# One-hots placed later on VectorE, more gathered rows issued by SyncE, and a joined end in a graph layer

## The chip, the cores and the metric

The kernel runs on one core of one Trainium2 chip. The engines of the core are TensorE (PE in the profile; PEld is its weight load), VectorE (DVE), ScalarE (ACT), GpSimd (POOL) and SyncE (SP), which only issues DMAs and waits. The metric is the device time of one launch in microseconds. Before the change it is 1567.36 us, the median of 3 runs (1563.31 to 1572.13).

## The reference

A graph layer with a residual and a layer norm. There are 6250 nodes with 64 features and 200000 edges, sorted by destination:

```python
w   = silu(edge_attr_32 @ W1 + b1) @ W2 + b2              # per edge, 9 weights
msg = einsum('ef,em,fmg->eg', x[src], edge_attr_9 * w, W_tp)
agg = segment_sum(msg, dst, 6250) / sqrt(16)
emb = silu(node_vec[:, None] @ Wn1 + bn1) @ Wn2 + bn2
gamma, beta = split(emb, 2, axis=-1)
y   = x + agg * (1 + gamma) + beta
out = (y - mean(y)) / sqrt(var(y) + 1e-5)                 # over the 64 features
```

## The kernel before

**Tiles and groups.** Edges come in tiles of 128 (one edge per partition), 1563 of them, and 16 tiles make a group (the last, group 97, has 11). There are 98 groups. Nodes come in 49 blocks of 128.

**The source rows.** For each tile the 128 rows `x[src]` have to lie in the tile `hs` of the group. There are three ways to get them. Most tiles are gathered by POOL with one indirect DMA each (`gather`, L91). Three or four tiles of each group are picked on PE (`pick`, L475): one-hot matrices `hot_k`, made on DVE from the keys (`hots`, L460), multiply a copy of `x` that stays in SBUF, in 14 matmuls per tile, and two DVE instructions (L484, L486) select the row out of the result. And the first tile of every sixth group from 7 on (`SPG`, 16 groups) is fetched row by row by SyncE: `load_rows` reads the source numbers from the SBUF tile `src_r` into registers, up to eight words with one register load (L101), and then issues one DMA of 256 bytes per row (L106). It does 22 rows (`SPR`) in each of the six steps before the group is used.

**A step.** The loop `for i in range(NBLK)` writes out the order by hand for all engines, and each engine takes its own instructions in that order. Step i starts the gathers of group i+6, loads edge data `ea` and `sh` for groups i+2 and i+3 (even i; L371, L373), keys (odd i; L391), and SyncE's rows, all in SyncE's one queue apart from the gathers. DVE makes the one-hots of group i+2 (two of them first, then the rest after the first pick). PE picks the tiles of group i+1; between the matmuls of the first pick it runs `nodes(i)`: the gate of a node block (L589, read by DVE in L355 and L356, until step 50), the placing of the sums of two groups on their nodes (`place`, L559, read by DVE in L565 and ACT in L568) in even steps, and the transposing back and the finish of two node blocks (`bring`, L576, and `finish_nodes`, L669 to L683) in every fourth step. Then come the hidden layer of group i+2 (`hidden`, L403, with the SiLU L411 on ACT), the second layer of group i+1 (`second`, L420), the edge sums of group i (`windows`, L504, copied out of PSUM by ACT in L514), in odd steps the product with `W_tp` for two groups (`project`, L543 or, for a single group, L538), and the remaining picks.

**Buffers that tie the engines.** PSUM tile `s` holds the results of `nodes` and then those of `second`, one after the other, so `second` waits until DVE and ACT have read what `nodes` left. PSUM tile `p1` holds the hidden layer and then the result of `project`, so `project` waits until ACT has applied the SiLU. `hs` has 7 buffers, `ea` and `sh` 3, `hot_k` 7.

**The end.** The last groups are 96 and 97. Groups 95 and 96 make a pair; group 97 stands alone. In the last step the pair is projected, placed, brought back and finished; then `windows(97)` and a second, shorter chain for group 97 follow.

Of the kernel before, what the change touches and what calls it, by code (L numbers as in the profile page):

```python
# [7 lines left out]
F32 = mybir.dt.float32  # L8
# [19 lines left out]
LB = 2  # L28
Q = 4
J = 7  # L30
SPG = range(7, NBLK, 6)
SPR = 22
EPS = 1e-5

KH = 8
# [9 lines left out]
def pair(q):  # L45

    return [g for g in (2 * q - 1, 2 * q) if 0 <= g < NBLK]
# [12 lines left out]
def gnn_resnorm_kernel(ctx: ExitStack, tc: tile.TileContext, x, src, dst, dst_row, ea, sh, cn,  # L60
# [18 lines left out]
    with ExitStack() as fast:  # L79
# [16 lines left out]
        src_r = keep.tile([len(SPG), P], I32)  # L96

        def load_rows(g, e0):
            for e in range(e0, min(e0 + SPR, P), 8):
                n = min(8, min(e0 + SPR, P) - e)  # L100
                _, vs = nc.values_load_multi_w_load_instructions(  # L101
                    src_r[SPG.index(g):SPG.index(g) + 1, e:e + n], engines=[mybir.EngineType.SP],
                    min_val=0, max_val=NPAD - 1,
                    skip_runtime_bounds_check_because="src is below N, as for the gathers")
                for k in range(n):
                    nc.sync.dma_start(hs[g][e + k:e + k + 1, 0, :], x[bass.ds(vs[k], 1), :])  # L106
# [27 lines left out]
        def setup(temp):  # L134
# [126 lines left out]
            def between(h):  # L261

                if h == 0:
                    p_f = psum.tile([KB, NBLK], F32, tag="s", name="p_f")
                    nc.tensor.matmul(p_f, first_t, ident[0:NBLK, 0:NBLK], start=True, stop=True)
                    nc.scalar.copy(first_f, p_f)
                elif h == 1:
                    keys(0)
                    hots(0, 0, Q)
                elif h == 3:  # L270
                    p_cn = psum.tile([P, NJ], F32, tag="s", name="p_cn")
                    nc.tensor.matmul(p_cn, cn_j, ident[0:NJ, 0:NJ], start=True, stop=True)
                    cn_s = temp.tile([P, NJ], F32)
                    nc.scalar.copy(cn_s, p_cn)
                    nc.sync.dma_start(cn_d, cn_s)
                    nc.sync.dma_start(wn1c, wn1.rearrange("o h -> h o"))
                    nc.sync.dma_start(bn1c, bn1.unsqueeze(1))
                    gate_load(0)
                    nc.sync.dma_start(wn2a[0:H, :], wn2)
                    nc.sync.dma_start(wn2a[H:H + 1, :], bn2.unsqueeze(0))  # L280
                    for q in range(2):
                        n = (M + 1 - q) // 2
                        nc.sync.dma_start(wtc2[q * F:(q + 1) * F, 0:n, :], wtp[:, q:M:2, :])
                    load(LB)
                    with nc.allow_non_contiguous_dma(reason="2048 words, once"):
                        nc.sync.dma_start(src_r, src[:, SPG[0] * KB:NBLK * KB:6 * KB].rearrange("p g -> g p"))


            for h in range(J):
# [67 lines left out]

        out_v = out.rearrange("(j p) f -> p j f", p=P)

        def finish(j0, j1, sums):  # L360
            y = late.tile([P, j1 - j0, F], F32, tag="y", name=f"y{j0}")
            finish_nodes(nc, late, eps, sums, y, gam[:, j0:j1, :], xb[:, j0:j1, :], out_v[:, j0:j1, :], j0)


        ea_t, sh_t, oh_t, kr_t, st, a, zs = {}, {}, {}, {}, {}, {}, {}
# [128 lines left out]
        def windows(g):  # L494

            nk = tiles(g)
            hsg, ag = hs.pop(g), a.pop(g)
            z = zs[g] if g in zs else sums(g)
            for k0 in range(0, nk, ZT):
                n = min(ZT, nk - k0)  # L500
                pz = psum.tile([P, ZT // 2, M, W], F32, tag="pz", name=f"pz{g}_{k0}", bufs=2)
                for k in range(n):
                    v = k % 2
                    mm = nc.tensor.matmul(pz[v * F:(v + 1) * F, k // 2].rearrange("p m w -> p (m w)"),  # L504
                                          hsg[:, k0 + k, :], ag[:, k0 + k].rearrange("p m w -> p (m w)"),
                                          start=True, stop=True)
                    if k0 + k == 0:

                        for d in hs_dma.pop(g)[(g not in SPG):]:
                            tc.add_manual_dep(mm.ins, d.ins.name, mybir.DependencyInfo(  # L510
                                mybir.DependencyClass.Sync, mybir.DependencyReason.DATA), reason="rows of the group")
                for v in range(2):
                    for h in range(2):
                        nc.scalar.copy(  # L514
                            z[h * F:(h + 1) * F, 0:5 - h, k0 + v:k0 + n:2, :].rearrange("p m k w -> p k m w"),
                            pz[v * F:(v + 1) * F, 0:(n + 1 - v) // 2, h:M:2, :])

# [12 lines left out]
        def project(q):  # L530


            gs = pair(q)
            pt = psum.tile([P, 2, 4 * P], F32, tag="p1", name=f"pt{q}")
            z = [zs.pop(g).rearrange("p c k w -> p c (k w)") for g in gs]
            if len(gs) == 1:
                for c in range(5):
                    nc.tensor.matmul(pt[:, 0, 0:F], z[0][:, c], wtc2[:, c, :], start=(c == 0), stop=(c == 4))  # L538
                halves(q, pt[:, 0, 0:F].unsqueeze(1))
                return []  # L540
            for c in range(5):
                for h in range(2):
                    nc.tensor.matmul(pt[h * F:(h + 1) * F, 0, 0:P], wtc2[:, c, :], z[h][:, c],  # L543
                                     start=(c == 0), stop=(c == 4))
# [6 lines left out]

            return [lambda: None, lambda: None, turn]

        def place(q, pd):

            gs = pair(q)

            def part(k):
                nc.tensor.matmul(pd, r[q][:, k].rearrange("p s f -> p (s f)"), hot.pop(gs[k]),  # L559
                                 start=(k == 0), stop=(k == len(gs) - 1))  # L560
                if k == len(gs) - 1:
                    r.pop(q)
                    if q > 0:
                        yt[q - 1] = work.tile([P, P], F32, tag="yt", name=f"yt{q}", bufs=3)
                        nc.vector.tensor_add(yt[q - 1], pd[:, 0:P], carry.pop(q - 1))  # L565
                    if q < NJ:
                        carry[q] = work.tile([P, P], F32, tag="carry", name=f"carry{q}")
                        nc.scalar.copy(carry[q], pd[:, P:2 * P])  # L568

            return [lambda k=k: part(k) for k in range(len(gs))]  # L570

# [28 lines left out]
        with tc.manual_schedule(), tc.tile_pool(name="temp", bufs=1) as temp:  # L600
            setup(temp)

            for i in range(NBLK):
                if i + AHEAD < NBLK:
                    gather(i + AHEAD)
                if i % LB == 0 and i + LB < NBLK:
                    if i > 0:
                        load(i + LB)
                    near(i + LB)
# [2 lines left out]
                if i % 4 == 3 and i + 1 < NJ:  # L612
                    gate_load(i + 1)
                for g in SPG:
                    if 0 < g - i <= AHEAD:
                        load_rows(g, (AHEAD - g + i) * SPR)
                if i + 2 < NBLK:
                    keys(i + 2)
                    hots(i + 2, 0, 2)
                pick(i + 1, 0, [nodes(i)])  # L620
                if i + 2 < NBLK:
                    hots(i + 2, 2, Q)
                if 3 <= i <= 5:
# [4 lines left out]
                    second(i + 1)  # L628
                if i < NBLK - 2:
                    windows(i)  # L630
                turn = project(i // 2) if i % 2 == 1 else []
                if i % 4 == 1 and i - 1 < NJ:
                    gate_hidden(i - 1)
                if i + 1 < NBLK:
                    pick(i + 1, 1, [weights(i + 1), turn])
                for t in range(2, Q):
                    pick(i + 1, t)
                if i == NBLK - 1:
                    for f in turn:
                        f()  # L640
                    ps = psum.tile([P, 4, P], F32, tag="s", name="ps_l")
                    for f in place(i // 2, ps[:, 0:2].rearrange("p a n -> p (a n)")):
                        f()
                    py = psum.tile([P, FB, F], F32, tag="r", name="py_l")
                    for f in bring(NJ - 3, NJ - 1, py):
                        f()
                if i >= NBLK - 2:
                    windows(i)
                if i == NBLK - 2:
                    sums(i + 1)  # L650
            project(NBLK // 2)
            ps = psum.tile([P, 4, P], F32, tag="s", name="ps_n")
            for f in place(NBLK // 2, ps[:, 0:2].rearrange("p a n -> p (a n)")):
                f()
            for f in bring(NJ - 1, NJ, psum.tile([P, 1, F], F32, tag="r", name="py_n")):
                f()


    bad_n = nc.values_load(flag_i[0:1, 0:1], min_val=0, max_val=4 * P,
# [3 lines left out]
                     gam, xb, eps, out)  # L663


def finish_nodes(nc, work, eps, sums, y, gam, xb, out, tag):

    n = y.shape[1]
    nc.vector.tensor_mul(y, sums, gam)  # L669
# [10 lines left out]
    nc.vector.reciprocal(var, var)  # L680
    o = work.tile([P, n, F], F32, tag="o", name=f"o{tag}")
    nc.vector.tensor_mul(o, y, var.unsqueeze(2).to_broadcast([P, n, F]))
    nc.sync.dma_start(out, o)  # L683


def general_path(tc, dram, x, dst_row, ea, sh, src_i, dst_i, w1bd, b1c, w2bd, b2r, wtc,
# [3 lines left out]
    with ExitStack() as ctx:  # L690
# [109 lines left out]
        for j0 in range(0, NJ, JC):  # L800
# [4 lines left out]
            nc.vector.tensor_add(a[0], a[0], a[1])  # L805
            nc.vector.tensor_add(a[2], a[2], a[3])
            nc.vector.tensor_add(a[0], a[0], a[2])
            finish_nodes(nc, work, eps, a[0], a[0], gam[:, js, :], xb[:, js, :], out_v[:, js, :], f"g{j0}")


# [47 lines left out]
```

## Time and profile before

| | us |
|---|---|
| median of 3 runs | 1567.36 |
| the profiled execution | 1570.09 |
| its span, first to last instruction | 1568.3 |
| PE busy in it | 1460.5 |
| POOL busy | 1129.5 |
| DVE busy | 1139.5 |
| ACT busy | 528.6 |

The profile is of one execution. Its page gives busy times by engine, the groups of instructions by line with their mean duration, and the idle time before them with what ended it. A row of the waits reads: who waited, for whom, microseconds in total, times, longest. A row of the timeline reads: start, duration, engine, line, operation, output and input, number of merged instructions, and in brackets the idle time of the engine before it and what ended it. `SPq` is SyncE's queue; its instructions are not counted as busy, so its load has to be worked out from its waits and from the spacing of its instructions. The mean granted clock of PE was 0.972 of full speed.

### The profile page before, as it was taken

How to read it: one execution, taken by the hardware profiler on the slowest of the kernel's cores; microseconds unless marked ns; L12 is line 12 of the kernel's file. 1: busy time of each engine (PE TensorE's matmuls, PEld its weight loads, DVE VectorE, ACT ScalarE, POOL GpSimd, SP SyncE). 2: the span in 40 equal slices, each digit the busy share in tenths (PEclk: the TensorE clock that was granted, in tenths of full speed). 3: DMA queues.
4: the chain of work that ended last, by engine and by line, in shares of the span. 5: the costliest groups of instructions: out<-in, count | busy, mean ns of one | idle time of the engine just before them, and what ended most of it. 6: DMA issues, size and time to landing. Idle time of an engine off the chain costs nothing.

```text
span 1568.3 us, 34363 instructions
## 1 busy us (share of the span) xinstructions
PE 1460.5 (93%) x10810; PEld 1208.6 (77%) x10810; DVE 1139.5 (73%) x1987; ACT 528.6 (34%) x1335; POOL 1129.5 (72%) x1201
## 2 busy tenths in 40 slices
PE   4998999999999999999999999999999999999995
PEld 2787778778787788787877877877877878778774
DVE  5686777777777777777777777777777677777773
ACT  4232242433332423332333323323233332333331
POOL 7777777777777777777777777777777777777700
PEclk9999999999999999999999999999999999999997
DMA  5321222222222222222222222222222222222200
GB/s 166 93 62 55 53 75 51 63 56 71 57 62 65 63 54 61 56 71 59 58 71 53 59 53 71 59 53 70 53 60 55 68 54 58 71 53 59 71 7 5
DMA packets 90939, 96.16 MB, mean 61 GB/s; under 512 B 37161, under 2 KB 51451, under 8 KB 90748
## 3 DMA queue, kind: packets, MB, share of 16 engines
q1 hardware_dynamic: 51842, 53.09, 11.5%
q0 software_dynamic: 38144, 39.14, 11.4%
q8 instruction: 88, 1.44, 0.4%
q10 hardware_dynamic: 762, 1.64, 0.3%
q14 instruction: 103, 0.84, 0.2%
HBM read 92.04 MB, written 1.73 MB: 60 GB/s over the span
## 4 chain that ended last, share of the span: by engine, by line
PE 51%; POOL 20%; DVE 13%; issue 8%; DMA 4%; ACT 3%; SPq 0%; DVEq 0%; POOLq 0%; ACTq 0%
PE px L475 37%; POOL hs L91 20%; DVE hot_k L460 5%; PE pz L504 5%; DMA hs<-in_x_dram,src_i 4%; PE pt L543 3%; PE p L420 2%; DVE xm L484 2%; DVE hs L486 2%; PE p L403 1%; PE p L430 1%; ACT L411 1%; ACT st L411 1%; DVE oh L382 1%; ACT carry L568 1%
## 5 line engine op out<-in xcount | busy, mean ns | idle before, releaser
L91 POOL DMA_INDIRECT hs<-in_x_dram,src_i x1192 | 1128.2, 946 | 364.0 <-issue 335.0
L475 PE MATMUL px<-xs,hot_k 128*128 128x448 f32 x4970 | 1100.8, 375 | 8.4 <-DVE xs L294 7.8
L475 PEld LDWEIGHTS px<-xs,hot_k 128*128 128x128 f32 x4970 | 903.3, 190 | 96.7 <-issue 12.2
L484 DVE SCALAR_TENSOR_TENSOR xm<-li,jl,px 128x448 f32<-128x448 f32 x355 | 240.4, 677 | 220.2 <-PE px L475 217.9
L460 DVE TENSOR_TENSOR hot_k<-pk,nk 128x896 fp32r<-128x896 f32 x355 | 370.5, 1081 | 2.3 <-ACT pk L454 2.3
L486 DVE TENSOR_REDUCE hs<-xm 128x64 f32<-128x448 f32 x355 | 220.1, 620 | 12.5 <-DVE xm L484 0.2
L514 ACT COPY zt<-pz 64x160 f32<-64x160 f32 (+2 forms) x784 | 213.3, 272 | 23.0 <-PE pz L504 13.9
L411 ACT ACTIVATE st<-p,b1c 128x1024 f32<-128x1024 f32 x98 | 109.2, 1114 | 296.1 <-PE p L403 295.8
L568 ACT COPY carry<-ps 128x128 f32<-128x128 f32 x48 | 12.7, 265 | 390.2 <-DVE yt L565 382.4
L436 DVE TENSOR_TENSOR p<-p,sh 128x72 f32<-128x72 f32 x196 | 47.3, 241 | 132.7 <-ACT rt L546 47.7
L504 PEld LDWEIGHTS pz<-a,hs 128*64 128x64 f32 x3126 | 110.6, 142 | 41.9 <-issue 38.4
L442 DVE TENSOR_TENSOR a<-oh,p 128x1152 f32<-128x1152 f32 x98 | 132.6, 1353 | 3.3
L504 PE MATMUL pz<-a,hs 128*64 128x72 f32 x3126 | 125.5, 236 | 1.1 <-DMA hs<-in_x_dram,src_i 0.6
L403 PE MATMUL p<-ea,w1bd 64*128 64x512 f32 x392 | 113.5, 656 | 0.0
L420 PEld LDWEIGHTS p<-st,w2p 128*32 128x32 f32 x784 | 16.6, 108 | 113.3 <-issue 52.7
L543 PE MATMUL pt<-zt,wtc 128*64 128x128 f32 x960 | 72.8, 305 | 27.7 <-ACT st L411 26.0
L420 PE MATMUL p<-st,w2p 128*32 128x256 f32 x784 | 63.7, 395 | 35.7 <-DVE xb L356 32.0
L543 PEld LDWEIGHTS pt<-zt,wtc 128*64 128x64 f32 x960 | 62.2, 157 | 29.7 <-ACT st L411 27.8
L679 ACT ACTIVATE var<-var,eps 128x2 f32<-128x2 f32 (+1 forms) x25 | 7.4, 296 | 220.5 <-DVE var L678 220.5
L430 PE MATMUL p<-ident,p2s 128*128 128x128 f32 x196 | 54.4, 278 | 0.0
L454 ACT CAST pk<-kr 128x384 f32<-128x384 f16 (+1 forms) x98 | 53.9, 550 | 1.5 <-DMA kr<-kd 1.4
L403 PEld LDWEIGHTS p<-ea,w1bd 64*128 64x128 f32 x392 | 30.2, 188 | 28.8 <-issue 27.9
(122 smaller groups left out, 530.0 us busy)
## 6 DMA issues: line engine op xcount, KB each, us to landing
hs<-in_x_dram SPq DMA_DIRECT2D x2048, 0.2 KB
ea<-in_ea_dram SPq DMA_DIRECT2D x49, 512.0 KB
hs<-in_x_dram,src_i POOLq DMA_INDIRECT x1192
kr<-kd SPq DMA_DIRECT2D x49, 256.0 KB
sh<-in_sh_dram SPq DMA_DIRECT2D x49, 144.0 KB
cb<-cn_d SPq DMA_DIRECT2D x12, 128.0 KB
out_dram<-o SPq DMA_DIRECT2D x24, 64.0 KB
gam<-in_x_dram ACTq DMA_DIRECT2D x2, 448.0 KB
```

The costliest lines, as they stand in the source:

```text
L91: hs_dma[g] = [nc.gpsimd.indirect_dma_start(out=hs[g][:, t - g * KB, :], out_offset=None, in_=x, in_offset=bass.IndirectOffsetOnAxis(ap=sr ...
L403: nc.tensor.matmul(p1[:, i, :], w1bd[i * 64:(i + 1) * 64, :], e[i * 64:(i + 1) * 64, :], start=True, stop=True)
L411: nc.scalar.activation(st[g], p1_t.pop(g), AF.Silu, bias=b1c)
L420: nc.tensor.matmul(p2[g][c * D:(c + 1) * D, 0, :].rearrange("p (i e) -> p i e", i=2), w2p, s[:, :, c * P:(c + 1) * P], start=True, stop=True)
L442: nc.vector.tensor_mul(a[g], oh_t.pop(g)[:, :, None, :].to_broadcast([P, KB, M, W]), sw.unsqueeze(3).to_broadcast([P, KB, M, W]))
L460: nc.vector.tensor_tensor(hot_k[g, t], pk_t[g][:, t, None, :].to_broadcast([P, J, P]), nk.unsqueeze(2).to_broadcast([P, J, P]), op=ALU.is_ ...
L475: nc.tensor.matmul(px.rearrange("p f l -> p (f l)"), hot_k[g, t][:, h, :], xs[i][:, h].rearrange("p f l -> p (f l)"), start=(h == 0 and i ...
L484: nc.vector.scalar_tensor_tensor(xm, li[:, None, :].to_broadcast([P, F, J]), jl[:, c:c + 1], px, op0=ALU.is_equal, op1=ALU.mult)
L486: nc.vector.tensor_reduce(hs[g][:, tiles(g) - q + t, :], xm, AX.X, ALU.add)
L504: mm = nc.tensor.matmul(pz[v * F:(v + 1) * F, k // 2].rearrange("p m w -> p (m w)"), hsg[:, k0 + k, :], ag[:, k0 + k].rearrange("p m w -> ...
L514: nc.scalar.copy(z[h * F:(h + 1) * F, 0:5 - h, k0 + v:k0 + n:2, :].rearrange("p m k w -> p k m w"), pz[v * F:(v + 1) * F, 0:(n + 1 - v) // ...
L543: nc.tensor.matmul(pt[h * F:(h + 1) * F, 0, 0:P], wtc2[:, c, :], z[h][:, c], start=(c == 0), stop=(c == 4))
```

## The change

Five things are changed, and nothing else in the computation. First, the first two one-hots of a step are issued on DVE behind the work of `nodes`: the list `more` is run within `pick` after the parts of `nodes(i)`. Second, SyncE fetches the first tile of every fifth group (19 groups), 26 rows a step in five steps, with up to 13 words per register load (two loads a step); POOL gathers three tiles fewer. Third, the stores of finished blocks are put on a list and issued at the head of the next step. Fourth, `place` reads the carry with ACT ahead of DVE's addition, and the single-group `project` uses the PSUM tile `r`. Fifth, at the end the edge sums of groups 96 and 97 are made one behind the other, with half of their PSUM copies on DVE, the three remaining tiles of group 97 ahead of its first eight; then both are projected, placed into one PSUM tile, and the last three node blocks are brought back, finished and stored at once.

```diff
-SPG = range(7, NBLK, 6)
-SPR = 22
+SPG = range(7, NBLK, 5)
+SPR = 26
...
         def load_rows(g, e0):
-            for e in range(e0, min(e0 + SPR, P), 8):
-                n = min(8, min(e0 + SPR, P) - e)
+            for e in range(e0, min(e0 + SPR, P), SPR // 2):
+                n = min(SPR // 2, min(e0 + SPR, P) - e)
...
+            o = finish_nodes(nc, late, eps, sums, y, gam[:, j0:j1, :], xb[:, j0:j1, :], j0)
+            stores.append(lambda: nc.sync.dma_start(out_v[:, j0:j1, :], o))
...
-            for k0 in range(0, nk, ZT):
+            for k0 in reversed(range(0, nk, ZT)) if nk < KB else range(0, nk, ZT):
...
-                        nc.scalar.copy(
+                        (nc.vector.tensor_copy if v and g >= NBLK - 2 else nc.scalar.copy)(
...
             if len(gs) == 1:
+                pr = psum.tile([P, 1, F], F32, tag="r", name=f"pr{q}")
...
-        def place(q, pd):
+        def place(q, pd, last=None):
...
+                if last:
+                    nc.tensor.matmul(pd[:, P:2 * P], r.pop(last)[:, 0].rearrange("p s f -> p (s f)"),
+                                     hot.pop(pair(last)[0])[:, 0:P], start=False, stop=True)
+                    yt[q] = work.tile([P, P], F32, tag="yt", name=f"yt{last}", bufs=3)
+                    nc.scalar.copy(yt[q], pd[:, P:2 * P])
+                else:
+                    carry[q] = work.tile([P, P], F32, tag="carry", name=f"carry{q}")
+                    nc.scalar.copy(carry[q], pd[:, P:2 * P])
+                if q > 0:
+                    yt[q - 1] = work.tile([P, P], F32, tag="yt", name=f"yt{q}", bufs=3)
+                    nc.vector.tensor_add(yt[q - 1], pd[:, 0:P], carry.pop(q - 1))
...
                 if i + AHEAD < NBLK:
                     gather(i + AHEAD)
+                while stores:
+                    stores.pop(0)()
...
                 for g in SPG:
-                    if 0 < g - i <= AHEAD:
+                    if 0 < g - i <= AHEAD and (AHEAD - g + i) * SPR < P:
                         load_rows(g, (AHEAD - g + i) * SPR)
+                more = []
                 if i + 2 < NBLK:
                     keys(i + 2)
-                    hots(i + 2, 0, 2)
-                pick(i + 1, 0, [nodes(i)])
+                    more = [lambda: hots(i + 2, 0, 2)]
+                pick(i + 1, 0, [nodes(i), more])
...
-                if i == NBLK - 2:
-                    sums(i + 1)
+
+            turn = project(NBLK // 2 - 1)
             project(NBLK // 2)
-            ps = psum.tile([P, 4, P], F32, tag="s", name="ps_n")
-            for f in place(NBLK // 2, ps[:, 0:2].rearrange("p a n -> p (a n)")):
+            for f in turn:
                 f()
-            for f in bring(NJ - 1, NJ, psum.tile([P, 1, F], F32, tag="r", name="py_n")):
+            ps = psum.tile([P, 2 * P], F32, tag="s", name="ps_n")
+            py = psum.tile([P, 3, F], F32, tag="r", name="py_n")
+            for f in place(NBLK // 2 - 1, ps, NBLK // 2) + bring(NJ - 3, NJ, py):
                 f()
```

## The prediction

> **What bounds the kernel now.** I read the page first (busy times), then the waits of PE, then the timeline of one second-half block, then, because the change gives it work, the waits of SyncE's queue and its register loads one by one.
>
> ```profile
> PE 1460.5 (93%) x10810; PEld 1208.6 (77%) x10810; DVE 1139.5 (73%) x1987; ACT 528.6 (34%) x1335; POOL 1129.5 (72%) x1201
> ```
> ```profile
> PE p L420 <- DVE xb L356: 32.0, 34, 2.2
> PE pt L543 <- ACT st L411: 26.0, 12, 2.2
> ```
> PE has the work: 1460.5 of 1568.3 us. Its idle time inside the run comes in two repeated gaps. Until block 50, `second` (L420) waits for DVE to finish reading the PSUM tile that it wants (xb L356): some 24 times 0.38 us and 11 times 2.1 us. After that, `project` (L543) waits 12 times 2.16 us for the SiLU L411, which frees its PSUM tile. The timeline shows why:
>
> ```profile
> 1450.76 2.08 DVE L460 TENSOR_TENSOR hot_k<-pk,nk 128x896 fp32r<-128x896 f32 x2
> 1452.75 0.28 DVE L669 TENSOR_TENSOR y<-ps,gam 128x128 f32<-128x128 f32 x1
> ...
> 1454.89 0.30 ACT L679 ACTIVATE var<-var,eps 128x2 f32<-128x2 f32 x1 [7.85 <-DVE var L678]
> 1455.21 1.28 ACT L411 ACT_TABLE_LOAD   x1
> 1456.50 1.11 ACT L411 ACTIVATE st<-p,b1c 128x1024 f32<-128x1024 f32 x1
> 1457.67 1.31 PE L543 MATMUL pt<-zt,wtc 128*64 128x128 f32 x20 [2.16 <-ACT st L411]
> ```
> Two one-hots (2.08 us) stand on DVE ahead of the finish chain, so ACT's root, the table load, the SiLU and PE are all late. The windows of the profile put the clock at 0.78 in 1457:1461 and 1.00 just before: a 2 us gap is often followed by some 3.4 us at half clock.
>
> POOL issues gathers without a pause (1192 of 0.95 us with 0.30 us between), but is off the path: its last gather (block 97) starts at 1493, and PE takes block 97 at 1550.5.
>
> SyncE is not on the page as an engine. Between its first row (57.1) and its last (1531.2):
>
> ```profile
> SPq L106 <- PE pz L504: 47.3, 15, 5.1
> SPq L683 <- DVE xb L356: 41.1, 11, 6.6
> SPq L683 <- DVE o L682: 38.6, 12, 5.8
> SPq L106 <- DVE hs L486: 4.5, 1, 4.5
> ```
> With three microseconds of small waits that is 134 us. So SyncE is occupied for 1474 - 134 = 1340 us: it has 9% of slack, and every `ea` load stands in the same queue behind the rows.
>
> **What SyncE's work costs.** Eight rows in a run, then single register loads (min/median/max ns; one instruction each):
>
> ```profile
> 1447.66 3.15 SPq L106 DMA_DIRECT2D hs<-in_x_dram  x8
> ```
> ```profile
> L101 SPq TENSOR_LOAD <-src_r x1: 732/732/732, 1440.3 to 1440.3; - x1
> L101 SPq TENSOR_LOAD <-src_r x1: 799/799/799, 1446.7 to 1446.7; - x1
> L101 SPq TENSOR_LOAD <-src_r x1: 997/997/997, 1450.8 to 1450.8; - x1
> L101 SPq TENSOR_LOAD <-src_r x1: 1932/1932/1932, 1457.2 to 1457.2; - x1
> L101 SPq TENSOR_LOAD <-src_r x1: 1987/1987/1987, 1462.6 to 1462.6; - x1
> L101 SPq TENSOR_LOAD <-src_r x1: 1567/1567/1567, 1468.0 to 1468.0; - x1
> L101 SPq TENSOR_LOAD <-src_r x1: 735/735/735, 1529.9 to 1529.9; - x1
> ```
> A row costs (3.15 - 0.23)/7 = 0.42 us. The loads are, in order, of words 0-7, 8-15, 16-21, 22-29, 30-37, 38-43, and (last line) 126-127. Eight words cost 0.73 or 1.93 us, by where they begin: words 0 and 8 lie on 16-byte bounds, words 22 and 30 do not. The slow ones fit 0.33 + 0.20 per word (2: 0.73, 6: 1.53, 8: 1.93); the quick ones fit the same with four words at the price of one (8: 0.73; 6 as 4+1+1: 0.93, measured 1.00). Traffic of the `ea` load just before does not explain it: the two-word load stands in the same kind of step and is cheap, and six quick words cost more than eight. I read it as: a start off a 16-byte bound is read word by word.
>
> **The change, part by part.**
>
> *One-hots behind the reads.* No instruction is added. In the 11 finish steps of the first half the chain starts 1.4 us earlier (it still waits for `bring`), so a gap of 2.1 leaves 0.7: 15 us. The 24 gaps of 0.38 go: 9 us. In the second half 1.87 of 2.16 goes, 12 times: 22 us. Fourteen half-clock stretches of 3.4 us cost about 1.6 each (estimate, half of 3.4): 22 us. Together up to 68 us of PE time, if nothing else is late. The one-hots are later by the 3 to 4 us of the chain, covered: they serve the next block's picks. What is late next, were PE free, is POOL.
>
> *Rows by SyncE.* POOL loses 3 gathers x 1.25 = 3.7 us. SyncE gains 3 groups x 128 = 384 rows x 0.42 = +161 us.
> Register loads: before, a group has 3 x (0.73 + 0.80 + 1.00) + 2 x (1.93 + 1.99 + 1.57) + (2.03 + 1.98 + 0.74) = 23.3 us, x16 = 373. After, a group has ten loads beginning at words 0, 13, 26, 39, 52, 65, 78, 91, 104, 117. Only 0, 52 and 104 are on a 16-byte bound. No row shows a 13-word load. Its bounds: below, three quick fours and a single, 0.33 + 4 x 0.20 = 1.1; above, 0.33 + 13 x 0.20 = 2.93 word by word. I take the upper end for the seven unaligned ones, since all four unaligned rows lie on that line, and 1.17 for the three others: 3 x 1.17 + 6 x 2.93 + 2.53 (11 words) = 23.6, x19 = 449. That is +76 for 98 loads fewer; each load less saves 0.1 of gaps, -10. At the lower end it would be about -150.
> The later issue of the stores leaves SyncE's queue as it was: a store stands ahead of the next block's loads in both. That ACT's carry now goes ahead of DVE's yt, and that the one-group project of block 1 writes another PSUM tile, I cost at nothing: the first swaps two reads of 0.27 and 0.28 us of one tile, the second happens once; without cover it is under 1 us.
> Sum on SyncE: 1340 + 161 + 76 - 10 = 1567 us, 16.5 us a step over 95 steps. PE needs 15.6 before and 14.9 with the gain. So SyncE becomes the bound, its waits vanish, and PE waits at `hidden` (L403) for `ea` every second step; the 68 us on PE are swallowed by that wait.
>
> *The Trainium skill, Runtime: NRT & Kernel Launch, section Instruction fetch mechanics, says that a register load costs about 200 ns a register even in bulk. The slope of the unaligned rows agrees (1.93 - 0.73 over six words); the aligned eight words at 0.73 do not. By that rule for all words the new loads would cost 19 x 128 x 0.2 = 486 us, and the sum on SyncE some 35 us more.*
>
> *The end.* Last row at 57.1 + 1567 = 1624. The last `ea` load heads step 94; between it and the last row lie two steps: 50 rows (21.0), loads 5.9 + 3.7, and the `sh` issue 0.5: 31. So it is issued at 1593, lands in about 4 (DMA share 0.73 until 1461 after an issue at 1456.2), and PE goes on at 1597. Before, PE stood there at 1500.2 and the span ended at 1568.3: 68.1 us. Of this the gap at 1518 with its slow clock goes (3.5), and the joined end saves about 6: one chain of project, turn, place, bring, finish in place of two (the second ran from 1554.8 to the end), while copies by DVE halve the ACT copies. Bounds for that: 3, if project's copies stay on the path, to 9. 1597 + 68.1 - 9.5 = 1656 span. The profiled execution lies 1.8 above its span (1570.1), so 1658 for one like it; it stood 2.7 above the median of 1567.4, so 1655 at the median. Forecast 1657 us.
>
> **The rivals.**
> 1. *13-word loads cheap* (1.1 each: a reader that only cares for length). SyncE then needs 1340 + 161 - 150 = 1351 and is no bound; PE would gain 68 and run into POOL, whose last gather lands at 1496.4 - 3.7 = 1493; from block 97's windows to the end some 17.5 (estimate: 17.8 before, with project 48 put behind it and the second chain dropped). 1493 + 17.5 + 1.8 = 1512. Speaks for it: the aligned rows. Against: the four unaligned 6- and 8-word rows. It decides where an unaligned load costs under 1.6 us.
> 2. *Partly word by word* (single words up to the bound, then fours: 7 reads, 1.73): SyncE 1340 + 161 - 75 = 1426, near PE's own pace; about 1535. Against: words 22-29 would then be 5 reads, 1.33, and took 1.93.
> 3. *Loads at about 2.3*: SyncE's delay and PE's gain cancel, 1567. It needs a number that no row lies near.
> 4. *The one-hots' later place makes DVE late for the picks*: slower by at most the chain, 3 us in 24 steps; DVE is idle 27%, so I give it nothing of its own.
>
> **How the numbers follow.** SyncE as the bound 0.86; rivals 1 and 2 0.06 and 0.05; rival 3 0.03. Under the forecast the row at 0.41 to 0.43, the load at 2.75 to 3.0 and the end at 3 to 9 give 1620 to 1685; 1600 to 1690 leaves out rivals 1 to 3 and little else. Within 0.5% is about what a measurement can tell from no change: faster 0.11, same 0.03, slower 0.86.
>
> **What would show it.** Right: 190 register loads with a median near 2.9 us; SyncE's waits for stores and hs near zero; its last row after 1600; PE's `hidden` waiting 2 to 4 us for `ea` in most even steps; the waits at L420 and L543 mostly gone. Wrong: loads near 1.2 us and a last row before 1500, with PE waiting for POOL's gathers at the end.

## The result, and the profile after

The changed kernel takes 1684.19 us (median of 4 runs, 1682.67 to 1685.13); the kernel before took 1569.74 us beside it (median of 4, 1563.31 to 1577.18). The ratio is 1.0726, with a 95% interval of 1.0676 to 1.0777: slower by 7.3%, 27 us above the forecast of 1657 and inside the range. The profiled execution took 1682.67 us, its span is 1680.8 us and the mean granted clock is 0.943.

On some of the chips that ran the experiments the kernel before itself took 2534 to 2577 us, so each ratio below is taken against the kernel before on the same chip, and that time is given with it.

The lines that answer to those of before come first. Part 4 of the page follows the chain of work that ended last and gives its shares of the span, by engine and by line. By engine, before:

```profile
PE 51%; POOL 20%; DVE 13%; issue 8%; DMA 4%; ACT 3%; SPq 0%; DVEq 0%; POOLq 0%; ACTq 0%
```

The busy times of the kernel after, and then its part 4:

```profile
PE 1491.3 (89%) x10810; PEld 1215.6 (72%) x10810; DVE 1136.1 (68%) x1985; ACT 526.0 (31%) x1326; POOL 1127.0 (67%) x1198
...
SPq 45%; PE 27%; issue 13%; DMA 5%; DVE 4%; POOL 3%; ACT 2%; DVEq 0%; ACTq 0%
SPq L106 26%; PE px L478 18%; SPq L101 16%; DMA ea<-in_ea_dram 4%; POOL hs L91 3%; PE pz L508 2%; PE p L406 2%; PE p L423 1%; PE pt L548 1%; DVE xm L487 1%; SPq L376 1%; SPq L374 1%; SPq L394 1%; DVE hs L489 1%; ACT L414 1%
```

PE does the same 10810 matmuls as before in 1491.3 us instead of 1460.5, and the rest of the span grew from 107.8 to 189.5 us: 30.8 + 81.7 = the 112.5 us by which the span grew. In the chain of before, SyncE's queue (SPq) had 0%. Now it has 45%, nearly all of it on two lines of `load_rows`: L106 issues the rows and L101 loads the registers.

The waits of PE after (total us, times, longest us):

```profile
PE p L406 <- DMA ea<-in_ea_dram: 134.3, 40, 6.3
...
PE p L423 <- DVE xb L356: 7.6, 11, 0.7
```

L406 is `hidden` (L403 before), L423 is `second` (L420 before). The wait of `second` fell from 32.0 us in 34 gaps to 7.6 in 11 gaps of 0.7, just as worked out for the one-hots' new place; the wait of `project` for the SiLU, 26.0 us before, is down to 2.0. In their place stands one wait that before did not have: 40 times 3.4 us for `ea` (on the page of before PE has no idle time ahead of L403).

The waits of SyncE's own queue after, between its first row (58.4) and its last (1646.1):

```profile
SPq L365 <- DVE hs L489: 0.8, 3, 0.3
SPq L376 <- DVE p L439: 0.4, 1, 0.4
SPq L374 <- PE px L478: 0.3, 1, 0.3
```

With five smaller rows they sum to 2.8 us, against 134.2 in the rows of before. SyncE is now occupied almost without a pause, for 1587.7 - 2.8 = 1585 us.

Its register loads (min/median/max ns, first and last start): all together, and then four of the ten of one group, which begin at words 0, 13, 52 and 117:

```profile
L101 SPq TENSOR_LOAD <-src_r x190: 1157/2908/3138, 56.7 to 1638.9; - x190
...
L101 SPq TENSOR_LOAD <-src_r x1: 1202/1202/1202, 1563.8 to 1563.8; - x1
L101 SPq TENSOR_LOAD <-src_r x1: 3007/3007/3007, 1571.1 to 1571.1; - x1
...
L101 SPq TENSOR_LOAD <-src_r x1: 1188/1188/1188, 1598.8 to 1598.8; - x1
...
L101 SPq TENSOR_LOAD <-src_r x1: 2606/2606/2606, 1638.9 to 1638.9; - x1
```

The 190 loads sum to 455.0 us (370.3 before, in 288 loads). Over the 19 groups the loads from words 0, 52 and 104 take 1.21, 1.22 and 1.21 us on average; the 13-word loads from the six other words take 2.93 to 2.98; the 11 words from word 117 take 2.56.

What that does to PE is to be seen in one stall near the end, first on PE, then on SyncE (timeline: start us, duration us; the run of rows is shown from 1611.99 on):

```profile
1617.75 2.08 PE L406 MATMUL p<-ea,w1bd 64*128 64x512 f32 x4 [4.83 <-DMA ea<-in_ea_dram]
1619.76 1.08 PE L423 MATMUL p<-st,w2p 128*32 128x256 f32 x8
```
```profile
1611.99 1.87 SPq L106 DMA_DIRECT2D hs<-in_x_dram  x5
1613.92 0.41 SPq L374 DMA_DIRECT2D ea<-in_ea_dram  x1
1614.38 0.46 SPq L376 DMA_DIRECT2D sh<-in_sh_dram  x1
```

The `ea` load is issued only when the rows ahead of it in the queue are out (1613.9). It lands 3.8 us later, PE has stood idle for 4.83 us, and then runs `hidden` and `second` at about half speed: 2.08 us for four matmuls that take 1.13 in the timeline of before, 1.08 for eight that take 0.64. By the granted clock in the trace there are 30 stretches at 0.5 after 140 us, against 15 before, and 17 of them last 6.8 us, where all of before but the one at the very end last 3.4. Inside them PE is busy for 130.4 us, against 54.6. If half of that time is lost, as 2.08 against 1.13 suggests, they cost 37.9 us more than before (an estimate): enough for all of the 30.8 us.

### The profile page after: what moved, and what is told of

It reads as the page before. It is cut to its first block, busy times and chain, and to the rows that moved or that the text cites. A ratio compares the mean times of both kernels' runs of the same rounds, so it can differ in the third digit from the quotient of the medians.

```text
span 1680.8 us, 35427 instructions
## 1 busy us (share of the span) xinstructions
PE 1491.3 (89%) x10810; PEld 1215.6 (72%) x10810; DVE 1136.1 (68%) x1985; ACT 526.0 (31%) x1326; POOL 1127.0 (67%) x1198
## 4 chain that ended last, share of the span: by engine, by line
SPq 45%; PE 27%; issue 13%; DMA 5%; DVE 4%; POOL 3%; ACT 2%; DVEq 0%; ACTq 0%
SPq L106 26%; PE px L478 18%; SPq L101 16%; DMA ea<-in_ea_dram 4%; POOL hs L91 3%; PE pz L508 2%; PE p L406 2%; PE p L423 1%; PE pt L548 1%; DVE xm L487 1%; SPq L376 1%; SPq L374 1%; SPq L394 1%; DVE hs L489 1%; ACT L414 1%
## 5 line engine op out<-in xcount | busy, mean ns | idle before, releaser
L406 PE MATMUL p<-ea,w1bd 64*128 64x512 f32 x392 | 134.7, 769 | 134.3 <-DMA ea<-in_ea_dram 134.3
L518 ACT COPY zt<-pz 64x160 f32<-64x160 f32 (+1 forms) x776 | 211.1, 272 | 36.5 <-PE pz L508 28.0
L508 PEld LDWEIGHTS pz<-a,hs 128*64 128x64 f32 x3126 | 127.1, 160 | 54.0 <-issue 50.0
L406 PEld LDWEIGHTS p<-ea,w1bd 64*128 64x128 f32 x392 | 34.6, 216 | 166.0 <-DMA ea<-in_ea_dram 149.4
L508 PE MATMUL pz<-a,hs 128*64 128x72 f32 x3126 | 142.6, 254 | 2.6 <-DVE zt L518 1.2
L423 PEld LDWEIGHTS p<-st,w2p 128*32 128x32 f32 x784 | 16.8, 116 | 99.7 <-issue 67.8
L423 PE MATMUL p<-st,w2p 128*32 128x256 f32 x784 | 75.3, 462 | 7.6 <-DVE xb L356 7.6
L548 PE MATMUL pt<-zt,wtc 128*64 128x128 f32 x960 | 61.7, 275 | 2.0 <-ACT st L414 2.0
L548 PEld LDWEIGHTS pt<-zt,wtc 128*64 128x64 f32 x960 | 52.3, 138 | 3.8 <-ACT st L414 3.8
```

The costliest lines, as they stand in the source:

```text
L406: nc.tensor.matmul(p1[:, i, :], w1bd[i * 64:(i + 1) * 64, :], e[i * 64:(i + 1) * 64, :], start=True, stop=True)
L518: (nc.vector.tensor_copy if v and g >= NBLK - 2 else nc.scalar.copy)(z[h * F:(h + 1) * F, 0:5 - h, k0 + v:k0 + n:2, :].rearrange("p m k w ...
```

## The experiments

The theory: SyncE's queue is the bound, and it is full because a register load whose first word does not lie on a 16-byte bound is read word by word. The rivals that the runs tell apart from it: that the 384 more rows alone fill the queue, whatever the loads cost; that the loads only get dearer by their length; and that the harm is done elsewhere, by the one-hots' later place or by the joined end.

### Only the alignment changed

The decisive run keeps everything of the change, its 13-word loads and its 384 more rows included, and moves only where each load begins. (The row of indices is filled by ten small DMAs at the start instead of one; the first row goes out at 62.0 instead of 58.4.) The row of 128 indices is spread over 160 words, so that the words 13k to 13k+12 stand from word 16k on:

```diff
-        src_r = keep.tile([len(SPG), P], I32)
+        src_r = keep.tile([len(SPG), 160], I32)
...
-                    src_r[SPG.index(g):SPG.index(g) + 1, e:e + n], engines=[mybir.EngineType.SP],
+                    src_r[SPG.index(g):SPG.index(g) + 1, e // 13 * 16:e // 13 * 16 + n], engines=[mybir.EngineType.SP],
...
-                        nc.sync.dma_start(src_r, src[:, SPG[0] * KB:NBLK * KB:5 * KB].rearrange("p g -> g p"))
+                        sv = src[:, SPG[0] * KB:NBLK * KB:5 * KB].rearrange("p g -> g p")
+                        for c in range(10):
+                            n = min(13, P - 13 * c)
+                            nc.sync.dma_start(src_r[:, 16 * c:16 * c + n], sv[:, 13 * c:13 * c + n])
```

> The run with aligned loads again. On the chips of the first seven runs the kernel before itself took 2534 and 2577 us, because PE and DVE there stand still for 5 to 10 us every 20 to 25 us, so that SyncE has hundreds of microseconds of slack and its queue can't be the bound. Theory, on a chip where the kernel before takes about 1570: as said for the first of these runs, about 1512, 225 us less occupied time on SyncE, its last row before 1500. Rival (384 more rows alone fill the queue): above 1570.

Measured: 1512.47 us (1511.51 to 1513.75), before 1563.94 on the same chip, ratio 0.9677 [0.9652, 0.9703]. The change went from 7.3% slower to 3.2% faster by where its loads begin. The loads of this kernel, and the busy times and the chain's shares by engine from its page:

```profile
L101 SPq TENSOR_LOAD <-src_r x190: 1148/1227/1582, 60.2 to 1457.7; - x190
```
```profile
PE 1437.8 (95%) x10810; PEld 1192.1 (79%) x10810; DVE 1135.4 (75%) x1985; ACT 523.5 (35%) x1326; POOL 1126.2 (74%) x1198
...
PE 64%; POOL 13%; issue 7%; DMA 5%; DVE 4%; SPq 4%; ACT 2%; DVEq 0%; POOLq 0%; ACTq 0%
```

The 190 loads sum to 237.0 us instead of 455.0. SyncE issues its last row at 1463.8; from its first (62.0) that is 1401.8, of which it waits 35.4, so it is occupied for 1366, 219 less than in the change as made, nearly all of it the 218 us of the loads, and is no bound. PE needs 1437.8 us, 53.5 less than in the change as made: with the stalls went the half-clock stretches (5 stretches are left after 140 us). What PE waits for now:

```profile
PE pz L511 <- DMA hs<-in_x_dram,src_i: 11.7, 8, 5.0
...
PE p L426 <- DVE xb L359: 7.6, 11, 0.7
```

L511 is `windows`, which takes the gathers that POOL issues. From the end of a group's last gather instruction to PE's first matmul of `windows` lie 36 us at the first group, 2 us at group 65, and 1.5 to 7 us from there to the end. PE is busy for 99 of every 100 us between 400 and 1000 us and for 94 to 96 after that, so PE sets the pace first, and from about 1000 us on PE and POOL go nearly in step. Rival 1 of the prediction, loads that are cheap, would have run into POOL and ended at 1512. It describes this kernel, and this version beats both kernels.

The same kernel also ran on a chip where the kernel before takes 2533.56 us:

> The changed kernel with one thing different: the source numbers lie in src_r at 16 words for every 13, so that each of the 190 register loads begins on a 16-byte bound. Rows, words and loads are as many as in the changed kernel. Theory (unaligned loads are read word by word, and SyncE's queue is the bound): a 13-word load falls from 2.95 to about 1.2 us, SyncE's occupied time by 7 x 1.7 x 19 = 225 us, its queue is no bound any more, and the time falls from 1684 to about 1512, where POOL's last gather sets the end; some 55 us below the kernel before. Rival 1 (a load of 13 words is slow by its length, or by the traffic around it): loads and time stay, 1684. Rival 2 (384 more rows alone fill the queue): loads get quick, but the time stays above 1570.

It took 2499.45 us there, ratio 0.987 [0.9814, 0.9927]: faster than before by 1.3%, but 39 us slower than the kernel without SyncE's part on the same chip (2460.01 us, ratio 0.9723 [0.966, 0.9785], below). So there the added rows cost time even with cheap loads. The trace shows one reason to expect it: SyncE stands still too. The step from one row to the next in a run takes 0.76 us on average, against 0.42 in the run above (the medians are 0.42 and 0.41), and a quarter of these steps take more than 1 us, where none does above. That makes SyncE's 2432 rows cost 1831 us instead of 1037. The expectations for such chips speak of hundreds of microseconds of slack on SyncE. Between its first and last row it waits 166 us in this run, and 265 without its part of the change. What the 39 us consist of stays open, and the times on these chips can't separate the price of the rows from the price of the loads.

### SyncE's part alone

The kernel before with only the 19 groups, the 26 rows and the 13-word loads (and the guard on the number of steps that they need); one-hots and end as before:

```diff
-SPG = range(7, NBLK, 6)
-SPR = 22
+SPG = range(7, NBLK, 5)
+SPR = 26
...
-            for e in range(e0, min(e0 + SPR, P), 8):
-                n = min(8, min(e0 + SPR, P) - e)
+            for e in range(e0, min(e0 + SPR, P), SPR // 2):
+                n = min(SPR // 2, min(e0 + SPR, P) - e)
...
-                    if 0 < g - i <= AHEAD:
+                    if 0 < g - i <= AHEAD and (AHEAD - g + i) * SPR < P:
```

> The kernel before with SyncE's part alone, a third time, for a chip where the kernel before takes about 1570. Theory: last row near 1646, time near 1690, and PE's waits for ea beside the old gaps before L420 and L543. Rival (one-hots or end cost something in the changed kernel): nearer to 1568 than to 1684.

Measured: 1692.46 us (1690.39 to 1694.14), before 1572.98, ratio 1.0772 [1.0718, 1.0826]. The whole slowdown is in this part. Its waits of PE:

```profile
PE p L403 <- DMA ea<-in_ea_dram: 93.1, 35, 6.5
PE pt L543 <- ACT st L411: 25.9, 12, 2.2
PE p L420 <- DVE xb L356: 25.1, 16, 2.3
```

This is the clearest picture of a gain that is swallowed. Here the one-hots are still in the old place and the two old gaps are still there (25.9 and 25.1 us); in the change as made they are gone (2.0 and 7.6), and the wait for `ea` is 134.3 instead of 93.1. What PE saved in one place it stood in the next, since the `ea` loads come at SyncE's pace: 41 us less in the two gaps, 41 us more for `ea`. Only about 8 us are left between the two (1684 against 1692, with intervals of the ratios that overlap). They lie at the end, where SyncE no longer sets the pace: from PE's last restart after a wait for `ea` to the end of the span are 71.88 us here and 63.05 there. The last row goes out at 1649.0 here and at 1646.1 there.

The same kernel on two chips where the kernel before takes 2577.04 and 2538.4 us:

> The kernel before with SyncE's part of the change alone: 19 groups, 26 rows a step, loads of 13 words. One-hots, stores and end are as before. Theory (SyncE's queue is the bound, and the gain on PE is swallowed by the wait for it): last row near 1646 as in the changed kernel, and about 1690, since only the old end of some 6 us more tells the two apart; the gaps before L420 and L543 are still there. Rival (SyncE's part is hidden, something else in the change costs): within 1% of 1568.

> The kernel before with SyncE's part alone, again, for a chip where the kernel before takes about 1570. Theory: SyncE's queue is the bound here too, so its last row stands near 1646 and the time near 1690: the 55 us that one-hots and end are worth by themselves do not show beside it. Rival (one-hots or end cost something in the changed kernel): nearer to 1568 than to 1684.

It took 2619.65 us, ratio 1.0158 [1.0047, 1.0269], and 2581.04 us, ratio 1.0174 [1.0114, 1.0234]. The sign is the same, the size is about a fifth. SyncE's queue is nearly full there too: between its first and last row it waits 79 and 65 us, and PE waits 39 and 35 us for `ea`. The aligned rows also cost 39 us on such a chip (above), so these two runs do not show what the alignment is worth, and why the size is smaller is not shown.

### Everything but SyncE's part

The changed kernel with the 16 groups, 22 rows and 8-word loads of before:

```diff
-SPG = range(7, NBLK, 5)
-SPR = 26
+SPG = range(7, NBLK, 6)
+SPR = 22
...
-            for e in range(e0, min(e0 + SPR, P), SPR // 2):
-                n = min(SPR // 2, min(e0 + SPR, P) - e)
+            for e in range(e0, min(e0 + SPR, P), 8):
+                n = min(8, min(e0 + SPR, P) - e)
...
```

> The changed kernel with SyncE's part undone, a third time, for a chip where the kernel before takes about 1570. Theory: POOL has three gathers more than with padded loads (1512), 3 x 1.25 = 3.7 us, and is the bound from the middle on: about 1516. Rival (the move of three tiles to SyncE is what brings the gain): well above, 1540 or more.

Measured: 1515.64 us (1514.72 to 1516.93), before 1566.01, ratio 0.9684 [0.9629, 0.9739]: the one-hots and the joined end alone are worth 50 us. Busy times and waits of PE:

```profile
PE 1434.3 (95%) x10810; PEld 1190.7 (79%) x10810; DVE 1136.0 (75%) x1985; ACT 523.4 (35%) x1326; POOL 1128.5 (75%) x1201
```
```profile
PE pz L508 <- DMA hs<-in_x_dram,src_i: 14.0, 8, 3.6
...
PE p L423 <- DVE xb L356: 7.8, 11, 0.8
```

PE is 26 us less busy than before for the same matmuls. As in the padded kernel PE now waits for POOL's gathers (14.0 us; on the page of before, all the idle time ahead of `windows` is 1.1 us), and POOL here issues three gathers more. Against this run the padded kernel, which moves those gathers to SyncE, is 3 us shorter by the medians and 1.4 by the spans; three gathers at POOL's pace of 1.25 would be 3.7. The two ran on different chips and their ratios' intervals overlap, so that gain fits but is not separated. Rival 4, that the later one-hots make DVE late for the picks, has nothing for it: the kernel with them is 3% faster.

Twice more on chips where the kernel before takes 2533.56 and 2538.4 us:

> The changed kernel with SyncE's part undone: 16 groups, 22 rows a step, loads of up to 8 words, as before. One-hots behind the reads, and the joined end, stay. Theory: about 1515, with the waits at L423 and L548 nearly gone, the half-clock stretches too, and POOL's last three gathers costing up to 4 us more than in the run with aligned loads. Rival (the one-hots' later place or the joined end makes it slower): above 1568.

> The changed kernel with SyncE's part undone, again, for such a chip. Theory: POOL has three gathers more than with padded loads (1512), 3 x 1.25 = 3.7 us, and is the bound from the middle on: about 1516. Rival (the move of three tiles to SyncE is what brings the gain): well above, 1540 or more.

2460.01 us, ratio 0.9723 [0.966, 0.9785], and 2462.66 us, ratio 0.9711 [0.9663, 0.9759].

### The one-hots alone

```diff
+                more = []
                 if i + 2 < NBLK:
                     keys(i + 2)
-                    hots(i + 2, 0, 2)
-                pick(i + 1, 0, [nodes(i)])
+                    more = [lambda: hots(i + 2, 0, 2)]
+                pick(i + 1, 0, [nodes(i), more])
```

> The kernel before with the one-hots alone placed behind the work of nodes. Theory: the gaps before L420 and L543 shrink from 63 us to under 20 and most half-clock stretches go; about 1515, held there by POOL's last gather at 1496 and the old end of 18 us behind it. The difference to the run without SyncE's part is what the joined end is worth: at most 9 us, and under 4 if POOL holds both. Rival: the picks wait for late one-hots, and the time is 1568 or more.

Measured, beside a kernel before of 2533.56 us: 2461.77 us, ratio 0.9695 [0.9613, 0.9778]. With the joined end added (the run just above, on the same chip) it was 0.9723 [0.966, 0.9785]. So on that chip the gain is the one-hots', and what the joined end adds is too small to be told apart; on a chip where the kernel before takes about 1570 the one-hots were not run alone. The joined end can be read from profiles on other chips: from the start of block 96's windows to the end of the span are 25.8 us before and 27.7 with SyncE's part alone (both with the old end), and 22.8 after, 22.2 in the padded kernel and 20.7 without SyncE's part (all with the joined end). So it is worth 3.0 to 7.0 us, by which of them are compared.

### The price of a load, by length and by first word

The disputed cost by itself: the kernel before, with 40 more register loads at its end, of 1 to 16 words, each length from the words 0, 1, 2 and 3 of a row of indices that is there anyway. A small row load into a spare tile follows each. Its total time says nothing here.

```diff
...
+    k = 0
+    for off in range(4):
+        for n in (1, 2, 3, 4, 5, 6, 8, 12, 13, 16):
+            _, vs = nc.values_load_multi_w_load_instructions(
+                dst_i[0:1, off:off + n], engines=[mybir.EngineType.SP], min_val=0, max_val=NPAD - 1,
+                skip_runtime_bounds_check_because="dst is at most N")
+            nc.sync.dma_start(look[:, k % 4, :], x[bass.ds(vs[n - 1], 1), :])
+            k += 1
```

> The kernel before with 40 register loads behind its last store: 1, 2, 3, 4, 5, 6, 8, 12, 13 and 16 words from each of the words 0, 1, 2 and 3 of a row, each followed by one row DMA into a spare tile. The whole is some 60 to 100 us longer, which says nothing; the durations of the loads do. Theory: from word 0, fours cost one read each and the rest one each (4: 0.5, 8: 0.75, 12: 1.0, 13: 1.2, 16: 1.2 us); from words 1, 2 and 3, 0.33 + 0.20 per word (4: 1.13, 8: 1.93, 13: 2.93, 16: 3.5). Rival (single words up to the bound, then fours): from word 1, 8 words take 3 + 1 + 1 reads, 1.33. Rival (length alone): no difference between the four starts.

Measured, in us, each figure one load (this run was on a chip where the kernel before takes 2533.56 us; the rows agree with the group means of the two kernels themselves, on a bound and off it: 8 words 0.79 to 0.80 and 1.89 to 1.96 before, 13 words 1.21 to 1.22 and 2.93 to 2.98 after):

| words | 1 | 2 | 3 | 4 | 5 | 6 | 8 | 12 | 13 | 16 |
|---|---|---|---|---|---|---|---|---|---|---|
| from word 0 | 0.53 | 0.69 | 0.89 | 0.59 | 0.77 | 0.98 | 0.76 | 0.97 | 1.21 | 1.17 |
| from word 1 | 0.55 | 0.69 | 0.94 | 1.10 | 1.30 | 1.50 | 1.89 | 2.70 | 2.90 | 3.50 |
| from word 2 | 0.50 | 0.70 | 0.90 | 1.10 | 1.30 | 1.50 | 1.90 | 2.70 | 2.90 | 3.50 |
| from word 3 | 0.50 | 0.70 | 0.90 | 1.10 | 1.29 | 1.50 | 1.90 | 2.70 | 2.89 | 3.49 |

Eight words from word 0 and from word 1, and 13 words from word 0 and from word 1, as the trace has them (min/median/max ns of a single load):

```profile
L663 SPq TENSOR_LOAD <-dst_i x1: 757/757/757, 2520.8 to 2520.8; - x1
L663 SPq TENSOR_LOAD <-dst_i x1: 1894/1894/1894, 2538.8 to 2538.8; - x1
...
L663 SPq TENSOR_LOAD <-dst_i x1: 1208/1208/1208, 2523.9 to 2523.9; - x1
L663 SPq TENSOR_LOAD <-dst_i x1: 2895/2895/2895, 2544.4 to 2544.4; - x1
```

From word 1, 2 or 3 the load costs 0.30 + 0.20 for each word, and which of the three does not matter. From word 0 each whole four costs about what one word costs, and the words left over cost 0.20 each: three words take longer than four, and 13 longer than 16. That the bound is one of 16 bytes, not 8 or 32, is to be seen from word 2 (byte 8), as dear as word 1, and from word 52 in the change as made (byte 208, no multiple of 32), as quick as word 0. The price is what the runs show; "read word by word" is the theory's picture of it. A reader that aligned itself first (rival 2) would take 8 words from word 1 as three singles, a four and a single: five reads, 1.33. It took 1.89. A reader that only cares for length (rival 1) would show no difference between the rows of the table.

### Two more of the loads in place

The kernel before with its rows of indices moved by one word, so that no load is aligned any more:

```diff
-        src_r = keep.tile([len(SPG), P], I32)
+        src_r = keep.tile([len(SPG), P + 4], I32)
...
-                    src_r[SPG.index(g):SPG.index(g) + 1, e:e + n], engines=[mybir.EngineType.SP],
+                    src_r[SPG.index(g):SPG.index(g) + 1, e + 1:e + 1 + n], engines=[mybir.EngineType.SP],
...
-                        nc.sync.dma_start(src_r, src[:, SPG[0] * KB:NBLK * KB:6 * KB].rearrange("p g -> g p"))
+                        nc.sync.dma_start(src_r[:, 1:P + 1], src[:, SPG[0] * KB:NBLK * KB:6 * KB].rearrange("p g -> g p"))
```

> The kernel before with src_r moved by one word, so that no load begins on a 16-byte bound; rows, words and loads are as before, 288 loads of 8, 6 and 2 words. Theory: the nine quick loads of a group go from 0.73, 0.80 and 1.00 to 1.93, 1.99 and 1.57 us, +8.9 us a group, +142 us in all; SyncE's occupied time goes from 1340 to about 1482, just over the 1474 us that it had, its waits vanish, and the time goes up by 10 to 35 us, to 1578 to 1603. Rival (slow loads come from the traffic of the even steps, or from length): no load changes, 1568.

The changed kernel with 28 rows a step in loads of 16 and 12 words, which all begin on a bound without any padding:

```diff
-SPR = 26
+SPR = 28
...
-            for e in range(e0, min(e0 + SPR, P), SPR // 2):
-                n = min(SPR // 2, min(e0 + SPR, P) - e)
+            for e in range(e0, min(e0 + SPR, P), 16):
+                n = min(16, min(e0 + SPR, P) - e)
```

> The changed kernel with 28 rows a step in loads of 16 and 12 words: every load begins on a 16-byte bound by its size, without padding, and there are 9 loads a group in place of 10. Theory: loads of 1.2 and 1.0 us, 190 us in all in place of 455, and the same time as with padded loads, about 1512. Rival (long loads are slow): 1684 or more.

Both ran on a chip where the kernel before takes 2577.04 us. First the shifted kernel's loads, then those of the one with 28 rows:

```profile
L101 SPq TENSOR_LOAD <-src_r x288: 3/1632/2134, 130.0 to 2546.3; - x144
```
```profile
L101 SPq TENSOR_LOAD <-src_r x171: 3/1028/1434, 129.5 to 2478.3; - x171
```

The loads went the way that was expected. Single durations scatter on these chips (the shortest are 3 ns), so sums are compared: 431 us for the shifted loads, against 293 for the same 288 loads unshifted on another such chip (the run with the one-hots alone), 138 more where 142 was expected; and 167 for the kernel with 28 rows, where 190 was expected. The times tell less. The shifted kernel took 2582.74 us, ratio 1.0016 [0.9979, 1.0053], where the expectation was 10 to 35 us more on a chip of 1570: SyncE still waits 227 us between its first and last row here, and PE does not wait for `ea`. On time this run is inconclusive. The kernel with 28 rows took 2555.97 us, ratio 0.9938 [0.99, 0.9976]: slightly faster than before; its interval overlaps that of the padded kernel on such a chip (0.987 [0.9814, 0.9927]). Whether it would reach 1512 on a chip like the forecast's is not shown.

## Why the prediction was right, and where it was off

The mechanism and the sign were right, step by step:

- **The price of the loads** was taken from four unaligned rows of 2, 6 and 8 words and carried to 13. Forecast: 1.17 on a bound, 2.93 off it, 2.53 for 11 words. Measured: 1.21, 2.93 to 2.98, 2.56. The sweep shows the rule, and the padded kernel shows that it decides the sign.
- **SyncE as the bound**: its waits all but vanished (2.8 us left), the last row came after 1600, and `hidden` waited for `ea` 40 times at 3.4 us on average, where 2 to 4 was forecast.
- **PE's gain swallowed**: up to 68 us were forecast. Without SyncE's part the gain is 50 us; with it about 8 remain, at the end. That the 50 fall short of 68 fits the 14.0 us for which PE now waits for gathers, as the first rival had it, but was not tested by itself. In the same runs the wait at `second` leaves 11 gaps of 0.7 us, as forecast.
- **Rival 1** was wrong as a forecast of this kernel and right as a sum: 1512 forecast for cheap loads, 1512.47 measured when they were made cheap. That it is so close is in part luck: PE takes block 97 at 1492.2 (1493 forecast), but from there to the end are 19.8 us and not 17.5, and the median lies 1.3 us below the profiled execution. Rival 2 and rival 4 are answered above. Rival 3 needed loads of 2.3 us, and no load of 13 words is near that.

The 27 us by which the point was too low come from two terms of the sum.

- **"Sum on SyncE: 1340 + 161 + 76 - 10 = 1567" was too small by 18.** It measured 1585. Five of the 18 were in the 1340 already: one of the waits taken off, 5.1 us long, ends at 57.1, where the first row begins, so it lies outside the 1474 us, and SyncE was occupied for 1345. The loads are 85 dearer than before (455.0 - 370.3) where 76 was written down, and with the pauses before them they are 80 dearer where 76 - 10 = 66 was: 14 more, so half of the 10 came. The rows came to 158 (161 forecast), and 2 us lie in SyncE's other instructions. With the first row 1.3 us later and 2.8 us of waits, the last row is 22 us later than forecast (1646 against 1624), and the last `ea` issue 21 (1613.9 against 1593). The landing was right: 3.8 us, 4 forecast.
- **"1597 + 68.1 - 9.5" left out the half clock after the last stall.** From PE's last restart to the end are 63.05 us (1617.75 to 1680.8), against 68.1 - 9.5 = 58.6. The run with SyncE's part alone, which has the old end behind the same kind of stall, takes 71.88 there: 3.8 more than the 68.1 of before, which had no stall at that place. Against it the change saves 8.8, where 9.5 was forecast for the gap at 1518 and the joined end together.

21 and 4.4 make the 25 us by which the span is longer than the forecast of 1656; the rest is that the forecast stood 1 us above its span and the measured median stands 3.4 above its own.

For the price of the loads the prediction weighed the Trainium skill: Runtime: NRT & Kernel Launch, section Instruction fetch mechanics, gives about 200 ns for a register, also in bulk. The page speaks of registers loaded from HBM; the loads here read a tile in SBUF. Off a bound the sweep agrees (0.20 for each word). On a bound it does not: 16 words in 1.17 us are 0.07 a word. The measurement decides, and the 172 us between the padded kernel and the change as made hang on that difference.

## What to carry to other kernels

An engine that only issues is not in the table of busy times; make its budget yourself, as the time from its first to its last issue less the waits that lie in it, before giving it more work, and ask which large load stands behind the small ones in its queue. Start a load of many registers on a 16-byte bound and take a multiple of four words, or pad the tile so that it does: here that is worth 172 us on the chips where the kernel before takes about 1570, a gain of 3% in place of a loss of 7%. A gain on the busiest engine is real only while no queue that feeds it is full, so what comes next (here SyncE, then POOL) is worked out in the same way as the bound itself.

## What the runs showed of the hardware that was not expected

- A register load of 13 words takes 2.90 us from word 1 and 1.21 from word 0, and one of 16 words from word 0 (1.17) is quicker than one of 5 words from word 1 (1.30). The prediction had read the effect of a bound from four rows; that it is the same from words 1, 2 and 3, with no attempt to align on the way, is the sweep's.
- A feeding queue that is late costs PE twice: the wait itself (134.3 us), and half-clock stretches behind it, 30 against 15 and more than half of them twice as long, by the estimate above enough for all of the 30.8 us by which the same matmuls took longer. In the kernel without the late queue there are 5 and PE is 23 us less busy than before.
- Some chips ran the same kernel before in 2534 to 2577 us. In the traces taken there PE, DVE and POOL stand still again and again (in the padded kernel's run PE 65 times after 200 us, for 4.5 to 12.3 us), and so does SyncE between its rows. In that run DVE waits for something that the profile can only call remote (waits of DVE: total us, times, longest us):

```profile
DVE xm L490 <- remote: 585.5, 103, 57.4
DVE xm L490 <- PE px L481: 164.5, 58, 6.5
```

What stops the engines there stays open. SyncE's part of the change costs 1.7% on such a chip in place of 7.7%, and rows with aligned loads cost about as much there (2499.45 us against 2460.01, 1.6%), so the price of the loads does not show in its times.
